# A graph-network kernel of four layers: layer 2's weight product in seven-product form, with the order of its last stage rearranged

## The chip, the cores and the metric

The kernel runs on one core of a Trainium2 chip. The metric is the device time of one execution in microseconds. Before the change three runs took 1876.82, 1876.82 and 1878.27 us.

The engines are named as in the profile: PE is TensorE (matmuls; PEld is its weight loads), DVE is VectorE, ACT is ScalarE, POOL is GpSimd, SP is the engine that issues DMAs. SBUF is the working memory, PSUM the eight banks that TensorE writes its results to.

## The reference

`x` holds 128 graphs of 64 nodes with 256 features, all f32. Four layers follow each other, each with a residual: `x = x + layer(relu(layernorm(x)))`. Layer 0 is two graph convolutions and four LSTM passes, layer 1 two products with batch norms. The change is in the code of layers 2 and 3:

```python
# layer 2: W is (3, 256, 256), adj (64, 64)
adj_0 = jnp.diag(jnp.diagonal(adj)); adj_1 = jnp.triu(adj, k=1); adj_2 = jnp.tril(adj, k=-1)
h = jnp.einsum('bjf,kfo->kbjo', x, W)
out = adj_0 @ h[0] + adj_1 @ h[1] + adj_2 @ h[2] + bias        # per graph
# layer 3: causal attention over the 64 nodes, one head of width 256
q, k, v = jnp.split(x @ Wqkv, 3, axis=-1)
attn = softmax(where(causal, q @ k.T / 16 + adj, -1e30))
out = (attn @ v) @ Wo
```

## The kernel before, in words

The 8192 rows (128 x 64) are cut into 16 supertiles of 512 rows, `s` = 0 to 15; a supertile is four tiles `q` of 128 rows, two graphs in each. The 256 features are two chunks `c` of 128. Layers 0 and 1 run first, up to about 1452 us. Layers 2 and 3 run together in the last stage, supertiles in pairs (an even and an odd one), by the function `rest`.

The order is written out by hand. `rest` calls `at(t, fn, ...)` for every step with a planned time; all steps of all pairs, each pair shifted by `PERIOD`, are sorted by that time and issued in that order. The times only fix the order: each engine runs its own instructions in it, and waits on semaphores for what they need. A step that is issued before another on the same engine therefore holds it up if it has to wait.

For one supertile the steps are:

- `load` (L1196) brings the residual `x1` back from DRAM through SP's queue. `affine` (L1200) finishes layer 1's batch norm on the transposed tiles `y`. `turn` (L1215) transposes them into PSUM, and `turned` adds `x1`: the result is `x2`.
- `norm` (L1226) is layernorm and relu: row statistics on DVE (`stats`), the inverse root on POOL (`root`), the shift on DVE (`shift`), and four relus on ACT, giving `h2`. `biased` (L1260) adds the layer's bias to `x2` on POOL.
- `graphs3` (L1263), four calls, multiplies each graph's 64 rows of `h2` by the three parts of the adjacency, which are packed beside each other (192 columns). Each call has four matmuls on half of the rows of the array and fills two PSUM banks; ACT and DVE copy one each. The result `ag` holds, transposed, three parts `m` of each chunk `c`: `ag[c, m, 512 rows]`.
- `weigh` (L1280) multiplies by the layer's weights: for each tile, six matmuls (two chunks, three parts) with a piece of `ag` as the stationary operand and 256 columns of `wl2[m]` moving. Every f32 matmul appears as two records in the trace. `weighed` adds `x2` and gives `x3`.
- A second `norm` gives `h3`; `h3` and `h3_copy` (L1293, L1301) transpose it. The score product is taken with one combined matrix, in a seven-product form that exists already: `qsum` (L1308) makes sums of the data, `qproduct` (L1319) the seven products with the weight sums `aqk` as the stationary operand, `qcopy` and `qadd` evict them. `hv` (L1344) is the value product.
- `scores` (L1356), `masked`, `largest`, `exps`, `turn_e`, `turned_e` are the softmax; `attend` (L1388) multiplies by the values in two halves of two tiles, and `attended` (L1394) scales the result, adds it into `x3` and, after the second half, issues the output DMA.

The steps of neighbouring supertiles are interleaved so that TensorE has the products of one to do while the other engines work on another. In the steady order of a pair the even and the odd supertile's `graphs3` stand next to each other, then follow the weight products of both, with the odd attention of the pair before, transposes and softmax pieces in between, and then both score products.

PSUM in this stage is one pool, `psum`, of eight banks, in which each new tile takes a bank that earlier steps have been done with, and waits for its last reader. Weights come by DMA in the stage before (`wl2` at L1137, three DMAs of 256 KB). The function `weight_sum` (L307) makes the four sums of a weight matrix that seven-product forms need: `S1 = A21 + A22`, `S2 = S1 - A11`, `S3 = A11 - A21` in A21's place, `S4 = A12 - S2`. It is used for the LSTM, layer 0, layer 1 and `aqk`.

Of the kernel before, what the change touches and what calls it, by code (L numbers as in the profile page):

```python
# [9 lines left out]
F32 = mybir.dt.float32  # L10
AF = mybir.ActivationFunctionType
# [3 lines left out]
P = 128  # L15
# [5 lines left out]
def kernel(ctx: ExitStack, tc: tile.TileContext, a: dict, out: bass.AP):  # L21
# [84 lines left out]
    nc.gpsimd.memset(mhalf, -0.5)  # L106
    eps = const.tile([P, 1], F32, tag="eps", name="eps")
    nc.gpsimd.memset(eps, EPS)
# [770 lines left out]
    def bn_coeffs(name, co, stats, c):  # L879


        prm = con[name]
        mv = lns.tile([P, 2], F32, tag=f"{name}mv{c}", name=f"{name}mv", bufs=1)
        nc.vector.bn_aggr(mv, stats[:, c, :, :].rearrange("p s k -> p (s k)"))
        scale, shift, v = (co[:, k, c : c + 1] for k in range(3))
        nc.gpsimd.tensor_add(v, mv[:, 1:2], eps)
        nc.gpsimd.tensor_tensor(v, v, mhalf[:, :1], ALU.pow)
        nc.gpsimd.tensor_mul(scale, v, prm[:, 1, c : c + 1])
        nc.gpsimd.tensor_mul(shift, mv[:, 0:1], scale)
        nc.gpsimd.tensor_sub(shift, prm[:, 2, c : c + 1], shift)  # L890
# [7 lines left out]
    with tc.tile_pool(name="pz", bufs=1, reuse_waits="tile") as pz:  # L898
# [237 lines left out]
        adj3, smask = adj4[:, 0:3, :], adj4[:, 3, :]  # L1136
        wl2 = [weight(f"wl2_{k}", a["W"][k], late) for k in range(3)]  # L1137
        bl2 = row_bcast("bl2", a["bias"], D, late)
# [4 lines left out]
        wo = weight("wo", a["Wo"], late)  # L1143

        with tc.tile_pool(name="tp", bufs=2, reuse_waits="tile") as tp_:
            tp.append(tp_)
            emit(1e9)
# [30 lines left out]


    PERIOD, HALF = 52.5, SUP // 2  # L1180
    NP = NS // 2
    with tc.tile_pool(name="pc", bufs=2, reuse_waits="tile") as pc, \
            tc.tile_pool(name="pc1", bufs=1, reuse_waits="tile") as pc1:
        events = []

        def rest(s, at, only_pair, t_T, t_n, t_G, t_W, t_h, t_QH, t_S, t_soft, t_E, t_O, end):
            first_, v = s == 0, {}
# [12 lines left out]
            def affine(c):  # L1200
                if s == 1:
                    nc.scalar.activation(y[c], y[c], AF.Identity, bias=co2[:, 1, c : c + 1],
                                         scale=co2[:, 0, c : c + 1])
                    return
                nc.vector.tensor_scalar(y[c], y[c], co2[:, 0, c : c + 1], co2[:, 1, c : c + 1],
                                        op0=ALU.mult, op1=ALU.add)

# [17 lines left out]

            def norm(src, tag, halves, t_rows, t_relu):  # L1226

                def new():
                    v["st"] = pc.tile([P, Q, 6], F32, tag="ln_st", name="ln_st", bufs=4)
                    v["mv"] = pc.tile([P, Q, 2], F32, tag="ln_mv", name="ln_mv", bufs=4)  # L1230
                    v["rn"] = pc.tile([P, 2, Q], F32, tag="ln_rn", name="ln_rn", bufs=4)
                    v[tag] = pc.tile([P, Q, D], F32, tag=tag, name=tag)

                def stats(q):
                    nc.vector.bn_stats(v["st"][:, q, :], v[src][:, q, :])
                    nc.vector.bn_aggr(v["mv"][:, q, :], v["st"][:, q, :])

                def root(qs):
                    rn = v["rn"][:, 0, qs]
                    nc.vector.tensor_scalar_add(rn, v["mv"][:, qs, 1], EPS)  # L1240
                    nc.gpsimd.tensor_tensor(rn, rn, mhalf[:, : qs.stop - qs.start], ALU.pow)  # L1241

                def shift(qs):
                    nc.vector.scalar_tensor_tensor(v["rn"][:, 1, qs], v["mv"][:, qs, 0], -1.0,  # L1244
                                                   v["rn"][:, 0, qs], op0=ALU.mult, op1=ALU.mult)

                def relu(q):
                    nc.scalar.activation(v[tag][:, q, :], v[src][:, q, :], AF.Relu,  # L1248
                                         bias=v["rn"][:, 1, q : q + 1], scale=v["rn"][:, 0, q : q + 1])

                at(t_rows[0] - 0.01, new)
                for q in range(Q):
                    at(t_rows[q // 2] + 0.6 * (q % 2), stats, q)
                for k, qs in enumerate((q2s(0), q2s(1)) if halves else (slice(0, Q),)):
                    at(t_relu[k] - 1.5, root, qs)
                    at(t_relu[k] - 0.1, shift, qs)
                    for q in range(qs.start, qs.stop):
                        at(t_relu[k] + 0.6 * (q - qs.start), relu, q)
# [20 lines left out]

            def weigh(k, q):  # L1280
                if q == 0:
                    v["W"] = two(bank())
                for n in range(3 * KC):
                    c, m = divmod(n, 3)
                    nc.tensor.matmul(v["W"][:, q, :], v["ag"][:, c, m, ts(2 * k + q, P)],  # L1285
                                     wl2[m][:, c, :], start=(n == 0), stop=(n == 3 * KC - 1))

            def weighed(k):
                if k == 0:
                    v["x3"] = pc.tile([P, Q, D], F32, tag="x3", name="x3", bufs=4)  # L1290
                nc.vector.tensor_add(v["x3"][:, q2s(k)], v["x2"][:, q2s(k)], v["W"])

# [15 lines left out]
            def qsum(k):  # L1308
                if k == 1:
                    v["t"] = sums_of.tile([P, 3, 512], F32, tag="th", name="tq").rearrange(  # L1310
                        "p k (n c) -> p (k n) c", c=HALF)
                t = v["t"]
                nc.vector.tensor_sub(t[:, k], *(None, (b_(0, 1), b_(0, 0)), (b_(1, 1), t[:, 1]),
                                                (b_(1, 1), b_(0, 1)), (b_(1, 0), t[:, 2]))[k])
# [4 lines left out]
            def qproduct(name, j):  # L1319
                new = ("q", name) not in v  # L1320
                if new:
                    v["q", name] = bank()[:, :HALF]
                if "qk" not in v:
                    v["qk"] = pc1.tile([P, KC, SUP], F32, tag="qk", name="qk")
                x_ = (b_(0, 0), b_(1, 0), b_(1, 1), *(v["t"][:, k] for k in (4, 1, 2, 3)))[j - 1]
                nc.tensor.matmul(v["q", name], aqk[:, OF[j], :], x_, start=new,  # L1326
                                 stop=(name, j) in (("a", 4), ("b", 3), ("c", 2)), skip_group_check=True)
# [7 lines left out]
            def qdirect(o):  # L1335
                if o == 0:
                    v["qk"] = pc1.tile([P, KC, SUP], F32, tag="qk", name="qk")
                p_ = bank()
# [66 lines left out]
            for c in range(KC):  # L1405
                at(t_T - (2 if first_ else 4.8 if s == 1 else 9) + (0.6 if s != 1 else 0.1) * c, affine, c)
            for k in range(2):
# [5 lines left out]
            if first_:  # L1413
                norm("x2", "h2", True, (t_T + 0.455, t_T + 1.8), (t_T + 3.2, t_T + 4.6))
                for q in range(Q):
                    at(t_T + 7 + 0.7 * q, biased, q)
            else:
                norm("x2", "h2", False, (t_n, t_n + 1.2), (t_n + (11.9 if s % 2 and s > 1 else 4.1),))
                for q in range(Q):
                    at(t_n + (18 if s % 2 else 10.5) + 0.7 * q, biased, q)  # L1420
            for k in range(4):
                at(t_G + 0.8 * k, graphs3, *((k % 2, k // 2) if first_ else (k // 2, k % 2)))
            for k in range(2):
                for q in range(2):
                    at(t_W[k] + 2.6 * q, weigh, k, q)
                at(t_W[k] + 5.3, weighed, k)
            norm("x3", "h3", False, (t_W[0] + 5.8, t_W[1] + 5.8), (t_W[1] + 8.8,))
            for c in range(KC):
# [35 lines left out]
            for k in range(2):  # L1464
                at(t_O + 0.86 * k, attend, k)
                at(t_O + 0.86 * k + 0.9, attended, k)

        for i in range(NP):
            t0, first_, end = PERIOD * i, i == 0, i == NP - 1

            def at(t, fn, *args, t0=t0):
                events.append((t0 + t, len(events), fn, args))

            rest(2 * i, at, i, -8.6 if first_ else -40.2, -38.3, 0, (7.0, 12.6), 29.0, 32.6, 40.0, 42.7,
                 46.3 if end else 48.46, 50.4 if end else 50.85, False)
            if first_:
                at(-7.6, weight_product, 2, wo, wvo)
                for k in range(8):
                    at(3.0 + 0.5 * k, qk_weights, k)
            rest(2 * i + 1, at, i, -3.0 if first_ else -27.6, 1.5 if first_ else -25.4, 12.3 if first_ else 3.5, (17.8, 26.5), 39.1,  # L1480
                 (42.0, 45.4, 48.7, 49.6, 52.1) if end else 42.0, 46.7 if end else 48.9,
                 49.5 if end else 59.5, 53.0 if end else 64.7, 53.8 if end else 75.6, end)
        for _, _, fn, args in sorted(events, key=lambda e: e[:2]):
# [40 lines left out]
```

## Time and profile before

| | us |
|---|---|
| median of three runs | 1876.82 |
| the profiled execution, its own time | 1876.78 |
| its span, first to last instruction | 1875.1 |
| last stage, from the first `graphs3` to the end | 413.6 (1461.46 to 1875.1) |
| of this: first pair, to the next pair's `graphs3` | 51.33 |
| six pairs, 1512.79 to 1818.09 | 305.30 |
| last pair and tail | 57.01 |
| PE busy in these six pairs | 305.30 of 305.30 |

The last four rows come from the trace's view by windows. A line of the profile that names a group gives the source line, the engine, the operation, `out<-in` with the names of the tiles, the sizes (partitions x elements), the count, and then the busy time, the mean length of one in ns, and the idle time ahead of it with what ended most of it. A line of the trace in order of time begins with start and length in us; a bracket at its end is the idle time ahead of it and who ended it. [...] the distance from start to start is its price in a stream.

### The profile page before, as it was taken

The page shows a single profiled execution, that of the slowest core. Times are in us where ns is not written, and L with a number is a line of the kernel's source. Part 1 is how long each engine was busy: PE and PEld are TensorE (multiplying, and loading weights), DVE is VectorE, ACT ScalarE, POOL GpSimd, SP SyncE. Part 2 cuts the span into 40 slices and gives each one's busy share as a digit, 9 for nine tenths or more (in the row PEclk, how much of TensorE's full clock was granted, in tenths as well). Part 3 has the DMA queues.
Part 4 walks back from the last instruction along what each step waited for, and adds up shares of the span by engine and source line. Part 5 has one row for each costly group of instructions (what it writes and reads, how often), then busy time and mean ns, then how long its engine had stood idle before and what let it go on. Part 6 is the DMA issues. An engine that isn't in the chain of part 4 may idle for free.

```text
span 1875.1 us, 19841 instructions
## 1 busy us (share of the span) xinstructions
PE 1853.9 (99%) x7080; PEld 1168.8 (62%) x7080; DVE 1129.4 (60%) x2254; ACT 925.7 (49%) x1594; POOL 645.4 (34%) x553
## 2 busy tenths in 40 slices
PE   8999999999999999999999999999999999999999
PEld 7997444444445666666444444566444788888887
DVE  6775777634546435445633333588876776667674
ACT  6776666534435334433533333378685434433442
POOL 4451422443424433422442222267353412211220
PEclk9999999999999999999999999999999999999999
DMA  4110001000001000000000000243200111111101
GB/s 146 57 57 1 1 1 29 16 1 0 1 0 45 1 0 1 1 1 1 23 0 0 1 0 0 102 132 116 71 1 2 44 46 46 35 46 46 46 23 34
DMA packets 50642, 54.86 MB, mean 29 GB/s; under 512 B 3184, under 2 KB 45936, under 8 KB 50544
## 3 DMA queue, kind: packets, MB, share of 16 engines
q1 hardware_dynamic: 50096, 53.30, 8.9%
q8 instruction: 56, 0.92, 0.2%
q14 instruction: 42, 0.34, 0.1%
q10 hardware_dynamic: 448, 0.30, 0.0%
HBM read 36.55 MB, written 17.04 MB: 29 GB/s over the span
## 4 chain that ended last, share of the span: by engine, by line
PE 93%; DVE 3%; POOL 1%; ACT 1%; DMA 1%; issue 1%; SPq 0%; ACTq 0%; DVEq 0%; POOLq 0%
PE ps L686 34%; PE ps L692 19%; PE ps L1285 8%; PE ps L930 5%; PE ps L1047 4%; PE ps L1350 3%; PE ps L392 3%; PE ps L402 3%; PE ps L1326 2%; PE ps L431 2%; PE ps L1273 2%; PE ps L1360 2%; PE ps L1391 1%; PE ps L623 1%; PE ps L1298 1%; PE ps L579 1%
## 5 line engine op out<-in xcount | busy, mean ns | idle before, releaser
L708 DVE TENSOR_TENSOR gate<-gate,ps 128x512 f32<-128x512 f32 (+2 forms) x378 | 223.9, 620 | 449.0 <-PE ps L692 367.7
L686 PE MATMUL ps<-tx,wih 128*128 128x512 f32 (+2 forms) x996 | 441.2, 541 | 1.9 <-ACT gate L711 1.0
L686 PE MATMUL ps<-hT,wih 128*128 128x512 f32 (+2 forms) x756 | 338.5, 541 | 0.0
L711 ACT COPY gate<-ps 128x512 f32<-128x512 f32 (+2 forms) x252 | 134.5, 534 | 378.4 <-PE ps L692 325.4
L686 PEld LDWEIGHTS ps<-tx,wih 128*128 128x128 f32 x996 | 188.4, 190 | 188.2 <-issue 128.2
L704 ACT ACTIVATE gate<-gate,lbias 128x512 f32<-128x512 f32 (+2 forms) x252 | 216.7, 860 | 160.0 <-DVE gate L708 160.0
L692 PE MATMUL ps<-h,whh 128*128 128x512 f32 (+2 forms) x576 | 256.6, 527 | 0.0
L686 PEld LDWEIGHTS ps<-hT,wih 128*128 128x128 f32 x756 | 143.6, 190 | 141.6 <-issue 79.4
L692 PE MATMUL ps<-th,whh 128*128 128x512 f32 (+2 forms) x432 | 192.5, 527 | 0.0
L731 POOL TENSOR_TENSOR gate<-gate 128x1024 f32<-128x1024 f32 (+2 forms) x36 | 71.9, 2019 | 297.5 <-ACT gate L704 297.5
L1285 PE MATMUL ps<-wl,ag 128*128 128x256 f32 x768 | 172.1, 380 | 0.0
L692 PEld LDWEIGHTS ps<-h,whh 128*128 128x128 f32 x576 | 109.4, 190 | 100.2 <-issue 76.5
L1285 PEld LDWEIGHTS ps<-wl,ag 128*128 128x128 f32 x768 | 143.4, 190 | 20.2 <-ACT ag L1278 1.8
L731 POOL TENSOR_TENSOR cell<-gate 128x1024 f32<-128x1024 f32 (+2 forms) x36 | 79.4, 2225 | 174.8 <-ACT gate L704 174.8
L1241 POOL TENSOR_TENSOR ln_rn<-ln_rn,mhalf 128x4 f32<-128x4 f32 (+1 forms) x33 | 32.8, 995 | 300.8 <-DVE ln_rn L1240 300.3
L692 PEld LDWEIGHTS ps<-th,whh 128*128 128x128 f32 x432 | 82.1, 190 | 75.2 <-issue 57.4
L1248 ACT ACTIVATE h<-x,ln_rn 128x256 f32<-128x256 f32 x128 | 68.2, 593 | 103.3 <-DVE ln_rn L1244 103.3
L731 POOL TENSOR_TENSOR cell<-gate,cell 128x1024 f32<-128x1024 f32 (+2 forms) x31 | 62.8, 2044 | 110.2 <-ACT gate L704 110.2
L711 DVE COPY gate<-ps 128x512 f32<-128x512 f32 (+2 forms) x126 | 78.6, 624 | 20.8 <-PE ps L692 20.8
L704 ACT ACTIVATE gate<-ps,lbias 128x512 f32<-128x512 f32 (+2 forms) x126 | 79.6, 631 | 3.8 <-PE ps L692 1.0
L736 ACT ACTIVATE gate<-cell 128x1024 f32<-128x1024 f32 (+2 forms) x72 | 68.0, 951 | 26.1 <-POOL cell L731 26.1
L648 DVE TENSOR_TENSOR tx<-hT,tx 128x512 f32<-128x512 f32 (+2 forms) x70 | 57.7, 825 | 13.8 <-PE ps L686 10.2
(236 smaller groups left out, 2933.8 us busy)
## 6 DMA issues: line engine op xcount, KB each, us to landing
xt<-in_x_dram SPq DMA_DIRECT2D x30, 512.0 KB, 4.2
x1d<-xt SPq DMA_DIRECT2D x16, 512.0 KB, 3.0
x<-x1d SPq DMA_DIRECT2D x16, 512.0 KB, 4.9
out_dram<-x SPq DMA_DIRECT2D x15, 512.0 KB, 3.0
wih<-in_WihT_dram SPq DMA_DIRECT2D x16, 256.0 KB, 4.8
whh<-in_WhhT_dram SPq DMA_DIRECT2D x12, 256.0 KB, 4.8
xt<-in_x_dram SPq DMA_DIRECT2D x6, 128.0 KB, 3.2
wl<-in_W_dram SPq DMA_DIRECT2D x3, 256.0 KB, 3.6
```

What stands on the lines that cost most here:

```text
L648: yield nc.vector.tensor_sub(t[k], *((b[1][0], b[0][0]), (b[1][1], t[0]), (b[1][1], b[1][0]), (b[0][1], t[1 % len(t)]))[k])
L686: nc.tensor.matmul(wide(p_[:, :N]), wih[0][:, OF[k], gi, :], x_, start=first_, stop=(j == 0), skip_group_check=True)
L692: nc.tensor.matmul(p_[:, :N], whh[0][:, OF[k], gi, :], h_, start=False, stop=True, skip_group_check=True)
L704: nc.scalar.activation(to, r[bank_][:, :N] if bank_ else to, fn, bias=lbias[:, l, m : m + 1])
L708: nc.vector.tensor_add(slot(n, hc), slot(n, hc), r[bank_][:, :N])
L711: op(slot(n, hc), r[bank_][:, :N])
L731: fn(*((t["G"] if isinstance(t, dict) and "G" in t else st["c"])[:, n, :, : st["N"]] for t in tiles))
L736: nc.scalar.activation(o_, c, AF.Tanh)
L930: nc.tensor.matmul(r[name], con["w1"][:, OF[j], g, :], x_, start=new, stop=(name, j) in (("a", 4), ("b", 3), ("c", 2)), skip_group_check=True)
L1047: nc.tensor.matmul(banks[name], w2[:, OF[j], k, :], x_, start=(new and k == 0), stop=(k == 1), skip_group_check=True)
L1248: nc.scalar.activation(v[tag][:, q, :], v[src][:, q, :], AF.Relu, bias=v["rn"][:, 1, q : q + 1], scale=v["rn"][:, 0, q : q + 1])
L1285: nc.tensor.matmul(v["W"][:, q, :], v["ag"][:, c, m, ts(2 * k + q, P)], wl2[m][:, c, :], start=(n == 0), stop=(n == 3 * KC - 1))
```

## The change

Layer 2's weight product of supertiles 1 to 15 takes a seven-product form. The two halves `n` of a supertile's rows and the two input chunks `c` are the blocks of the data, the two input and two output halves of 128 the blocks of the weights; each block holds the three adjacency parts, and a product sums over them. The four data sums (`gsum`, 128 x 768 each) are made on POOL, two of them in place. They are the stationary operand, 128 columns of weights (or weight sums) the moving one. A product `gproduct` is six matmuls (two tiles, three parts). Products 1, 6, 7 and 4 accumulate one after the other into one bank `a`, which is read after each of them; `b` and `c` hold the others. `gevict` and `gadd` put the quarters of `x3` together on DVE. Supertile 0 takes the old sums, in matmuls of 128 columns (`gdirect`).

With it:

- `wl2` becomes one tile of seven blocks, loaded by four DMAs; three of its weight sums are made on POOL during layer 1's second product, the last one after supertile 0 has read what it overwrites.
- PSUM is split in this stage: one bank for `a`, two for `b` and `c`, five for the rest. The score product uses the same `a` and `bc` banks.
- The even and the odd `graphs3` are two groups now: the even one, then two even weight products, then the odd one.
- The second half of the odd attention moves behind the fourth weight product of the odd supertile, the first half ahead of the even one's. The even attention's second eviction moves behind the `graphs3` evictions.
- In `norm`, adding epsilon and the shift move from DVE to POOL. `qsum` moves from DVE to POOL. `affine` moves from DVE to ACT and is planned earlier, except for supertile 0. The transposes of the next pair move to later places: among the score products.
- `qk` takes the place of `wqkv`, the data sums that of `wT`, both read for the last time before.

```diff
-        wl2 = [weight(f"wl2_{k}", a["W"][k], late) for k in range(3)]
+        wl2 = late.tile([P, 7, 3, P], F32, tag="wl2", name="wl2")
+        for o in range(2):
+            for c in range(2):
+                nc.sync.dma_start(wl2[:, 2 * o + c], a["W"].rearrange(
+                    "m (c p) (o n) -> o c p m n", c=2, o=2)[o, c])
...
+        for k in range(4):
+            if k != 2:
+                at(B + 60 + 5.16 * k, weight_sum, wl2, k)
...
+    new_banks(a=1, bc=2, psum=5)
...
                 def root(qs):
-                    rn = v["rn"][:, 0, qs]
-                    nc.vector.tensor_scalar_add(rn, v["mv"][:, qs, 1], EPS)
-                    nc.gpsimd.tensor_tensor(rn, rn, mhalf[:, : qs.stop - qs.start], ALU.pow)
+                    rn, nm = v["rn"][:, 0, qs], v["rn"][:, 1, qs]
+                    n = qs.stop - qs.start
+                    nc.gpsimd.tensor_add(rn, v["mv"][:, qs, 1], eps[:, :n])
+                    nc.gpsimd.tensor_tensor(rn, rn, mhalf[:, :n], ALU.pow)
+                    nc.gpsimd.tensor_mul(nm, v["mv"][:, qs, 0], rn)
+                    nc.gpsimd.tensor_mul(nm, nm, mone[:, :n])
...
-            def weigh(k, q):
-                if q == 0:
-                    v["W"] = two(bank())
-                for n in range(3 * KC):
-                    c, m = divmod(n, 3)
-                    nc.tensor.matmul(v["W"][:, q, :], v["ag"][:, c, m, ts(2 * k + q, P)],
-                                     wl2[m][:, c, :], start=(n == 0), stop=(n == 3 * KC - 1))
+            def g_(c, n):
+                return v["ag"][:, c, :, ts(n, HALF)]
+
+            def gsum(k):
+                if k == 0:
+                    v["t2"] = late.tile([P, 3 * KC, D], F32, tag="wT", name="tg")
+                t1, t2 = v["t2"][:, 0:3], v["t2"][:, 3:6]
+                if k == 0:
+                    nc.gpsimd.tensor_sub(t1, g_(0, 1), g_(0, 0))
+                elif k == 1:
+                    nc.gpsimd.tensor_sub(g_(0, 1), g_(1, 1), g_(0, 1))
+                elif k == 2:
+                    nc.gpsimd.tensor_add(t2, g_(0, 1), g_(0, 0))
+                else:
+                    nc.gpsimd.tensor_sub(g_(1, 0), g_(1, 0), t2)
+
+            def gproduct(name, j):
...
+                for p_ in range(2):
+                    for m in range(3):
+                        nc.tensor.matmul(v["g", name][:, p_, :], x_[:, m, ts(p_, P)], wl2[:, OF[j], m, :],
...
-                nc.vector.tensor_sub(t[:, k], *(None, (b_(0, 1), b_(0, 0)), (b_(1, 1), t[:, 1]),
+                nc.gpsimd.tensor_sub(t[:, k], *(None, (b_(0, 1), b_(0, 0)), (b_(1, 1), t[:, 1]),
...
             for k in range(2):
-                at(t_O + 0.86 * k, attend, k)
-                at(t_O + 0.86 * k + 0.9, attended, k)
+                at(t_O[k], attend, k)
+                at(t_O[2 + k], attended, k)
...
-            rest(2 * i, at, i, -8.6 if first_ else -40.2, -38.3, 0, (7.0, 12.6), 29.0, 32.6, 40.0, 42.7,
-                 46.3 if end else 48.46, 50.4 if end else 50.85, False)
+            rest(2 * i, at, i, -8.6 if first_ else -14.5, -12.5, 0,
+                 (7.0, 9.6, 12.2, 14.8) if first_ else (7.0, 8.3, 9.6, 10.9, 12.2, 13.5, 15.8),
+                 (3.3, 5.2, 7.1, 9.0), (12.5, 17.5) if first_ else (17.4, 15.3), 20.5, 25.75, 31.4, 40.0, 42.7,
+                 46.3 if end else 48.46, (50.4, 51.26, 51.3, 52.16) if end else (50.85, 51.71, 51.75, 55.4), False)
...
-            rest(2 * i + 1, at, i, -3.0 if first_ else -27.6, 1.5 if first_ else -25.4, 12.3 if first_ else 3.5, (17.8, 26.5), 39.1,
+            rest(2 * i + 1, at, i, -3.0 if first_ else -6.05, 1.5 if first_ else -5.2,
+                 12.25 if first_ else 9.0, (17.85, 19.6, 20.9, 22.2, 23.5, 24.8, 26.9),
+                 (16.0, 17.0, 18.0, 22.0) if first_ else (12.3, 14.2, 16.1, 22.0), (31.4, 30.6), 35.3, 39.1,
```

## The prediction

> **What bounds the kernel now.** I read the page first: busy time, then the chain that ended last, then TensorE in order of time over one period of the last stage, the only stage that the change rearranges.
>
> ```profile
> PE 1853.9 (99%) x7080; PEld 1168.8 (62%) x7080; DVE 1129.4 (60%) x2254; ACT 925.7 (49%) x1594; POOL 645.4 (34%) x553
> PEclk9999999999999999999999999999999999999999
> PE 93%; DVE 3%; POOL 1%; ACT 1%; DMA 1%; issue 1%; SPq 0%; ACTq 0%; DVEq 0%; POOLq 0%
> ```
>
> TensorE is busy 99% of the span at the full granted clock and holds 93% of the chain. In this kernel a microsecond is gained only by fewer TensorE microseconds, and lost by any wait of TensorE. The period of one pair of supertiles:
>
> ```profile
> 1614.55 5.47 PE L1273 MATMUL ps<-adj,h 64*128 64x192 f32 x64
> 1619.95 5.45 PE L1285 MATMUL ps<-wl,ag 128*128 128x256 f32 x24
> ...
> 1626.55 10.53 PE L1285 MATMUL ps<-wl,ag 128*128 128x256 f32 x48
> 1636.91 1.89 PE L1391 MATMUL ps<-hw,eT 128*128 128x256 f32 x8
> ...
> 1652.05 1.25 PE L1298 MATMUL ps<-ident,h 128*128 128x128 f32 x8
> 1653.13 1.95 PE L1360 MATMUL ps<-h3T,qk 128*128 128x128 f32 x16
> 1654.91 1.03 PE L1326 MATMUL ps<-h3T,aqk 128*128 128x256 f32 x4
> ...
> 1665.44 5.47 PE L1273 MATMUL ps<-adj,h 64*128 64x192 f32 x64
> ```
>
> Columns: start, length, engine, line, operation, operands, count of records. [...] Each f32 matmul is two records. The period is 1665.44 - 1614.55 = 50.89 us, with no marked idle. A 256-column record costs (1636.91 - 1626.55) / 48 = 0.216 us; a 128-column record with a new stationary tile each time (the scores) costs (1654.91 - 1653.13) / 16 = 0.1115, 1.79 / 16 = 0.112 in other periods. I take 0.1117.
>
> **Matmuls removed and added.** Before, a supertile's weight product has 24 matmuls, 48 records: 48 x 0.216 = 10.36 us. After, supertiles 1 to 15 have 7 products x 2 token tiles x 3 parts = 42 matmuls of 128 columns, 84 records: 84 x 0.1117 = 9.38 us, 0.98 less. Supertile 0 does the old sums in 48 matmuls of 128 columns: 96 x 0.1117 = 10.72, 0.36 more. Together 15 x -0.98 + 0.36 = **-14.3 us**. One eighth fewer columns would be 19.4 us; a quarter of it is eaten because two 128-column records cost 0.223 against 0.216.
>
> [...] The scores row is this very stream, in f32, and shows 0.112. I take the row.
>
> **Waits that the change adds on TensorE, per pair.** PSUM is split into one bank for the running accumulation, two for the others, and five for all else. During the even supertile's adjacency products one of the five is held by the second attention half, whose eviction now stands on VectorE behind four copies, so these products rotate in four banks.
>
> ```profile
> 1615.51 0.48 ACT L1278 COPY ag<-ps 128x384 f32<-128x384 f32 x1 [4.21 <-PE ps L1273]
> 1615.55 0.56 DVE L1278 COPY ag<-ps 128x384 f32<-128x384 f32 x1 [0.87 <-PE ps L1273]
> ```
>
> Against the first call's start (1614.55) the ACT copy ends at 1.44, the VectorE copy at 1.56. A call takes 5.40 / 8 = 0.675. The third call is ready at 1.35 and starts at about 1.51 (a released TensorE started 0.05 to 0.1 late): 0.16 lost. The first product reads what the third call made; its copies now end at about 3.07, TensorE is ready at 2.87: 0.27 lost. Before, the other supertile's adjacency products covered this. The odd group waits about 0.11 for an ACT copy, since four relus (2.07) and three exps (0.39 each) are queued ahead of it. Sum 0.54 per pair. Bounds: 0 if the copies land first; 1.5 if each odd copy is late by a whole exp.
>
> What goes with the old order: 0.1 before the first weight records (5.28 for 24 against 5.18) and 0.2 in the L1298 group (1.08 against 0.87), which now has transposes ahead of it: -0.3.
>
> **GpSimd's queue.** It takes over four data sums per supertile (128x768), the four sums of the attention product, and the norm's root and shift.
>
> ```profile
> L591 POOL TENSOR_TENSOR xt<-xt,h 128x512 f32<-128x512 f32 x24 | 30.1, 1276 | 0.0
> L1261 POOL TENSOR_TENSOR x<-x,bl 128x256 f32<-128x256 f32 x64 | 48.1, 777 | 10.7 <-ACT h L1248 10.7
> L1241 POOL TENSOR_TENSOR ln_rn<-ln_rn,mhalf 128x4 f32<-128x4 f32 x31 | 31.4, 1014 | 296.5 <-DVE ln_rn L1240 296.5
> L610 POOL TENSOR_TENSOR ln_rn<-ln_rn 128x4 f32<-128x4 f32 x16 | 3.2, 201 | 1.3
> ```
>
> From 256 (0.70 to 0.78) and 512 (1.28) columns a 768-column sum is about 1.83. Walking the queue from the even adjacency start: four even sums 2.3 to 9.6, four bias adds (0.73) to 12.5, three odd sums to 17.9. The odd sixth product needs the third at 20.6: 2.7 us spare. The root is now 0.2 + 1.01 + 0.2 + 0.2 with gaps, 1.85 against about 1.45; its relus end near 23.1, their transposes start at 24.7. Of the fourth sums the odd one is done at 22.9, needed at 25.5. All covered, and the price beyond the cover is the excess, once per pair.
>
> Contention is the unknown. This case shows it on VectorE:
>
> ```profile
> 1645.42 0.42 DVE L1313 TENSOR_TENSOR tq<-h3T,tq 128x256 f32<-128x256 f32 x1
> ...
> 1655.30 0.94 DVE L1313 TENSOR_TENSOR tq<-h3T 128x256 f32<-128x256 f32 x1
> ```
>
> The second ran beside GpSimd's bias adds. [...] By the worst such row (1.60 for 512 columns beside VectorE sums) a 768 sum would be 2.3, and the spare 2.7 would be overdrawn by 0.6. [...] I take 1.83.
>
> **Moves at nothing.** VectorE loses four sums (0.42 to 0.94) and two affines (0.53) a supertile and gains seven evictions (about 0.4) for two of 0.68; each eviction of the single accumulation bank must end within one product (1.34) and its queue leaves 0.1 to 0.7. ACT gains the affines (0.76) in stretches where it idles. The closest meeting: the copy of the transposed exponentials waits behind three row statistics and ends as attention is ready; 0.1 per pair is set down. The weight load is four DMAs instead of three, long landed; three weight sums of about 1 us fall in GpSimd's idle (27.0 us over seven pairs) during the second product.
>
> **SP's queue.** The second half of the odd attention moves from 1636.9 (22.4 us into the period) to about 27 us. Its output store now stands on SP ahead of the next pair's two loads, which came at 4 and 17 us of a period before and are needed from 34.9. Released at 28.8, a load lands 4.9 later by its row, at 33.7: 1.2 spare. [...] if a whole store (3.0) comes first, it lands at 36.7, 1.8 late, of which TensorE sees 1.4, since the copies of h3T queue behind it on VectorE with 0.4 spare. Nearest is the lone-load row; I set down 0.1 and keep 0 and 1.4.
>
> **The sum against the profiled execution** (1876.78; span 1875.1; the median of the runs, 1876.82, is the same). Six middle pairs: -1.96 + 0.54 + 0.1 (eT) + 0.1 (load) - 0.3 = -1.52, so -9.1. First pair: -0.62; +0.3 root; +0.3 adjacency; the sixth product waits on GpSimd, where one more weight sum stands ahead of two data sums, +0.87; the 0.79 wait for h3T goes: +0.1. Last pair: -1.96 + 0.54 - 0.1, and +0.4 because no transposes cover the slower root there: -1.1. In all -10.1: **1866.7 us**.
>
> **Rivals.** (1) *No new wait*, 0.14: copies land before TensorE needs their banks: -14.3 - 7 x 0.3 + 0.4 = -16.0, 1860.8. For: no wait in the present trace is over 0.3 us in the middle pairs; against: 1.44 after 1.35. (2) *Evictions pace TensorE*, 0.20: or the late load does: each of eight adjacency calls waits 0.15 and one product 0.2, or the load's 1.4 is seen, in seven pairs: 1866.7 + 9.8 = 1876.5. For: four banks for eight copies, three 512 KB transfers at once; against: VectorE's copies repeat every 0.49. (3) *GpSimd ends on the other side*, 0.09: with sums of g us the odd third sum ends at 5.2 + 7g. The 1.52 gain is gone when that passes 20.6 by 1.52, at g = 2.42; at 2.6 it passes by 2.8, a loss of 1.3 per pair: 1876.8 + 7 x 1.3 - 1 = 1885. For: the 1.60 row; [...] The built program does hold 630 + 48 matmuls, so doing nothing is no case.
>
> **Numbers.** Forecast's own case, 0.55: 1863 to 1871. Cases (1) and most of (2) belong in the range: 1860 to 1876. A change is told from none beyond 0.2%, 3.8 us: faster below 1873.1. Case (2) is split 0.09 faster, 0.10 same, 0.01 slower, case (3) 0.02 same, 0.07 slower: faster 0.78, same 0.12, slower 0.10.
>
> **What would show it.** Right: the period at 49.2 to 49.5; product records at 0.112; TensorE idle with releaser L1286's copies, about 0.5 per pair, in the third call and the first product. Wrong: product records over 0.12; idle released by GpSimd's data sums, which would then be over 2.2 us each; or accumulating products waiting for their evictions.

## The result and the profile after

The changed kernel takes **1868.99 us** (median of five runs, 1868.89 to 1869.76), the kernel before beside it 1877.69 (1876.82 to 1878.27): ratio 0.9955, 95% interval 0.9941 to 0.9970. It is faster by 0.45%; the forecast was 1866.7, in a range from 1860 to 1876.

The profiled execution took 1868.99, its span is 1867.2, against 1876.78 and 1875.1 before.

| | before | after | forecast change | change |
|---|---|---|---|---|
| up to the last stage | 1461.46 | 1460.82 | 0 | -0.64 |
| first pair | 51.33 | 51.57 | +0.1 | +0.24 |
| six pairs | 305.30 | 298.28 | -9.1 | -7.02 |
| last pair and tail | 57.01 | 56.53 | -1.1 | -0.48 |
| span | 1875.1 | 1867.2 | -10.1 | -7.9 |

The first pair needs a caution. The view by windows, the first pair before, then the first pair and the six middle pairs of the changed kernel, whose window ends 0.02 early (length, then busy time of PE, PEld, DVE, ACT and POOL, the granted clock of TensorE, and DMA):

```profile
1461.46:1512.79 51.33, 50.37 (x297) 43.22 (x297) 37.70 (x98) 22.86 (x52) 19.42 (x30) 1.00 0.04 11
```

```profile
1460.82:1512.39 51.57, 51.39 (x380) 47.47 (x380) 28.97 (x78) 24.07 (x52) 32.98 (x54) 0.97 0.04 11
1512.39:1810.65 298.26, 297.71 (x2281) 277.78 (x2280) 194.79 (x505) 136.37 (x336) 192.51 (x241) 1.00 0.13 43
```

The granted clock of 0.97 comes from a stretch of 3.4 us at 0.50, which the profiled execution of the kernel before did not have. The middle pairs ran at 1.00 in both, so the versions are compared by their periods below.

The page of the changed kernel, busy time and the new group of product records:

```profile
PE 1846.8 (99%) x7668; PEld 1179.0 (63%) x7668; DVE 1097.1 (59%) x2175; ACT 943.4 (51%) x1622; POOL 817.2 (44%) x777
...
L1314 PE MATMUL ps<-wl,ag 128*128 128x128 f32 x900 | 108.3, 276 | 0.6
```

TensorE still fills the span; GpSimd has taken over 172 us of work and VectorE has lost 32. TensorE in order of time, from the first adjacency call of a period:

```profile
1562.11 3.17 PE L1281 MATMUL ps<-adj,h 64*128 64x192 f32 x32
1565.37 2.92 PE L1314 MATMUL ps<-wl,ag 128*128 128x128 f32 x24
1568.22 3.05 PE L1281 MATMUL ps<-adj,h 64*128 64x192 f32 x32
1571.19 2.94 PE L1314 MATMUL ps<-wl,tg 128*128 128x128 f32 x24
...
1611.82 1.41 PE L1281 MATMUL ps<-adj,h 64*128 64x192 f32 x14
```

Read from start to start, since a length runs past the next start (1565.37 + 2.92 = 1568.29, and the next group starts at 1568.22), the period is 1611.82 - 1562.11 = 49.71, 1.18 less, where 1.52 was forecast. The 64 adjacency records of a pair took 1619.95 - 1614.55 = 5.40 in one group before. Now the even 32 take 3.26 and the odd 32 take 2.97, 6.23 together. The product records have the price that was taken. Later in the period 36 of them take 1581.97 - 1577.96 = 4.01, 0.1114 each:

```profile
1577.96 4.18 PE L1314 MATMUL ps<-wl,ag 128*128 128x128 f32 x36
1581.97 2.84 PE L1314 MATMUL ps<-wl,tg 128*128 128x128 f32 x24
```

So the loss sits in and around the adjacency groups, and no line there carries a bracket. It shows in another view, the waits of the weight loads (PEld), here for the six middle pairs of the changed kernel: engine, line, who it waited for, us in all, times, longest.

```profile
PEld ps L1314 <- ACT ag L1286: 2.1, 6, 0.4
PEld ps L1281 <- issue: 2.0, 6, 0.3
PEld ps L1314 <- issue: 1.3, 6, 0.2
PEld ps L1281 <- ACT ag L1286: 1.2, 6, 0.2
```

Two of the four rows say "issue": TensorE stood and waited for nothing that the profile shows. One is the step into the even adjacency group, one the step out of the odd group into products. The other two are the even third call (0.2) and the first product behind the even group (0.4). The same view of the kernel before, over its six middle pairs, had been there to be read:

```profile
PEld ps L1273 <- issue: 2.3, 7, 0.3
PEld ps L1298 <- ACT h L1248: 1.4, 6, 0.2
PEld ps L1285 <- ACT ag L1278: 1.3, 6, 0.2
```

The step into a group is there (0.3), and the step out, with the copies named as releaser; the middle row is the old wait of the L1298 transposes.

**A ledger of one period.** Each run of equal records is set against its count times the undisturbed price (0.1117 at 128 columns, 0.216 at 256, 0.0813 for an adjacency record, since two run side by side, 0.007 apart, and a pair of them comes every 0.163). What is over, in us:

| | before | after |
|---|---|---|
| steps into and out of the (even) group | 0.39 | 0.39 |
| even group: third call waits for banks | 0 | 0.31 |
| first product waits for the third call's copies | 0 | 0.13 |
| steps into and out of the odd group | no such group | 0.39 |
| odd group: third call waits for a bank | 0 | 0.18 |
| transposes of h3 (L1298) | 0.21 | 0 |
| sum | 0.60 | 1.40 |

A group that nothing holds up still costs 0.39: the last 256-column record ahead of it is followed after 0.309 instead of 0.216 (0.09), the group itself takes 0.20 over its records, and the first product record behind it takes 0.10 more. Products: 2 x (9.38 - 10.37) = -1.97. With +0.80 that is -1.17, the measured change.

### The profile page after: what moved, and what is told of

It reads as the page before. It is cut to its first block, busy times and chain, and to the rows that moved or that the text cites. A ratio compares the mean times of both kernels' runs of the same rounds, so it can differ in the third digit from the quotient of the medians.

```text
span 1867.2 us, 21317 instructions
## 1 busy us (share of the span) xinstructions
PE 1846.8 (99%) x7668; PEld 1179.0 (63%) x7668; DVE 1097.1 (59%) x2175; ACT 943.4 (51%) x1622; POOL 817.2 (44%) x777
## 4 chain that ended last, share of the span: by engine, by line
PE 94%; DVE 2%; POOL 1%; ACT 1%; issue 1%; DMA 0%; SPq 0%; DVEq 0%; POOLq 0%; ACTq 0%
PE ps L688 34%; PE ps L694 19%; PE ps L1314 7%; PE ps L932 5%; PE ps L1049 4%; PE ps L394 3%; PE ps L404 3%; PE ps L1401 3%; PE ps L1281 3%; PE ps L433 2%; PE ps L1377 2%; PE ps L1411 2%; PE ps L1442 1%; PE ps L625 1%; PE ps L1349 1%; PE ps L581 1%
## 5 line engine op out<-in xcount | busy, mean ns | idle before, releaser
L1314 PE MATMUL ps<-wl,ag 128*128 128x128 f32 x900 | 108.3, 276 | 0.6
L1314 PEld LDWEIGHTS ps<-wl,ag 128*128 128x128 f32 x900 | 104.2, 192 | 3.3 <-ACT ag L1286 2.5
L733 POOL TENSOR_TENSOR cell<-cell,gate 128x1024 f32<-128x1024 f32 (+2 forms) x31 | 65.5, 2135 | 0.4
```

Source lines behind the costliest of these rows:

```text
L733: fn(*((t["G"] if isinstance(t, dict) and "G" in t else st["c"])[:, n, :, : st["N"]] for t in tiles))
L1314: nc.tensor.matmul(v["g", name][:, p_, :], x_[:, m, ts(p_, P)], wl2[:, OF[j], m, :], start=new and p_ == m == 0, stop=m == 2 and (name, j) ...
```

## The experiments

Theory A: TensorE pays about 0.39 us for each group of 64-row adjacency matmuls among its 128-row ones, in and out, whoever waits. Theory B, the rival: all of the loss is waiting for PSUM banks and their evictions, and goes with them. The medians, the period in the profiled execution, and the ratio to the kernel before:

| | median us | period us | ratio, 95% interval |
|---|---|---|---|
| before, measured beside each | 1876.63 to 1877.69 | 50.89 | |
| changed | 1868.99 | 49.71 | 0.9955 (0.9941 to 0.9970) |
| two_groups_before | 1881.84 | 51.63 | 1.0025 (1.0015 to 1.0035) |
| three_groups | 1870.35 | 49.93 | 0.9964 (0.9952 to 0.9977) |
| full_rows | 1884.15 | 51.70 | 1.0035 (1.0021 to 1.0049) |
| six_banks | 1868.85 | 49.79 | 0.9956 (0.9944 to 0.9969) |
| a1_first | 1873.34 | 50.36 | 0.9979 (0.9973 to 0.9986) |
| no_waits | 1872.20 | 50.25 | 0.9972 (0.9961 to 0.9982) |
| no_waits2 | 1862.93 | 49.10 | 0.9926 (0.9914 to 0.9939) |
| one_group | 1867.16 | 49.55 | 0.9944 (0.9931 to 0.9956) |
| one_group2 | 1860.53 | 48.71 | 0.9915 (0.9901 to 0.9928) |
| order_only | 1885.92 | 52.13 | 1.0046 (1.0033 to 1.0059) |
| double_sum | 1875.64 | 50.59 | 0.9993 (0.9985 to 1.0001) |

**Two groups in the kernel before.** One planned time is moved:

```diff
-            rest(2 * i + 1, at, i, -3.0 if first_ else -27.6, 1.5 if first_ else -25.4, 12.3 if first_ else 3.5, (17.8, 26.5), 39.1,
+            rest(2 * i + 1, at, i, -3.0 if first_ else -27.6, 1.5 if first_ else -25.4, 12.3 if first_ else 9.5, (17.8, 26.5), 39.1,
```

> The kernel before with one edit: in pairs 1 to 7 the second supertile's four adjacency calls run behind the first quarter of the first supertile's weight product instead of directly behind the first supertile's calls. Same instructions, eight PSUM banks, no seven-product form. Theory A (a change of TensorE between 128-row and 64-row matmuls costs about 0.2 us each way, whatever waits there are): the period grows by 0.39 from 50.89 to about 51.28, and the kernel by 7 x 0.39 = 2.7, to about 1880.4. Theory B (the loss in the changed kernel's second group is a wait for PSUM banks and their evictions): with eight banks nothing waits, the period stays at 50.9 and the time within 0.5 us of 1877.7.

The four odd calls are planned 0.8 apart, so the next quarter of the product, planned at 9.6, fell between the first and the second: three groups, not two. TensorE of that kernel:

```profile
1615.42 2.87 PE L1273 MATMUL ps<-adj,h 64*128 64x192 f32 x32
1618.22 2.86 PE L1285 MATMUL ps<-wl,ag 128*128 128x256 f32 x12
1621.01 0.92 PE L1273 MATMUL ps<-adj,h 64*128 64x192 f32 x8
1621.86 2.86 PE L1285 MATMUL ps<-wl,ag 128*128 128x256 f32 x12
1624.64 2.22 PE L1273 MATMUL ps<-adj,h 64*128 64x192 f32 x24
1626.80 0.44 PE L1381 MATMUL ps<-ident,sc 128*128 128x128 f32 x2
```

Eight records take 0.85 where 0.65 is their price, 24 take 2.16 where 1.95 is, 32 take 2.80 where 2.60 is, and 12 product records between two groups 2.79 where 12 x 0.216 = 2.59. The overhead is the same for 8, 24 and 32 records (and for 64 before), with eight banks and nothing to wait for: a price per group. Two groups more at 0.39 are 0.78; the last one steps out into transposes, where the second record is 0.05 less late than among products; the period is 0.74 longer. Theory B had said 0.

**Three groups in the changed kernel.** The fifth product goes between the second and the third odd call:

```diff
-at(t_G + (... else 0.05 if s % 2 else 0.8) * k, graphs3, ...)
+at(t_G + (... else (0.05 * k + 1.7 * (k // 2)) / max(k, 1) if s % 2 else 0.8) * k, graphs3, ...)
```

> The changed kernel with the odd supertile's four adjacency calls split in two and two: the fifth product (b5) stands between them. One more group per pair. Theory A (each group costs 0.39 us for the change of matmul rows and back): +0.39, less the 0.17 that the third odd call now waits for its bank, +0.22 per pair in pairs 1 to 7, the period 49.93 instead of 49.71, 1870.5. Theory B (the second group loses time to evictions): the split gives the evictions 1.3 us more, so 0.17 to 0.5 per pair is gained, the period 49.2 to 49.5, 1865.5 to 1867.8.

The period is 49.93, as theory A said, and the time 1870.35. The 0.18 of waiting went, and the third group's 0.39 outweighed it: 0.22 more in all.

**Full rows.** The odd groups are multiplied as 128-row matmuls, both blocks at once:

```diff
+                if s % 2:
+                    full = [bank()[:, : 3 * P].rearrange("p (k n) -> p k n", k=3) for _ in range(2)]
+                    for q in range(2):
+                        nc.tensor.matmul(full[q], v["h2"][:, 2 * k + q, ts(c, P)], adj3, start=True, stop=True)
...
+                    return
```

> The changed kernel with the odd supertiles' adjacency products as 128-row matmuls: each takes both 64-row blocks at once against the block-diagonal matrix, 384 columns, so the two halves no longer run side by side. 16 records of about 0.324 us instead of 32 that take 2.60 together: +2.58. Theory A (the loss is the change of matmul rows): the odd group's steps in and out, 0.39 together, vanish, as does its bank wait of 0.17: +2.0 per pair, period 51.7. Theory B (any group of matmuls whose results others evict pays on entry and exit): the steps stay, +2.4, period 52.1.

```profile
1616.96 3.17 PE L1289 MATMUL ps<-adj,h 64*128 64x192 f32 x32
1620.22 2.92 PE L1322 MATMUL ps<-wl,ag 128*128 128x128 f32 x24
1622.97 5.33 PE L1279 MATMUL ps<-adj,h 128*128 128x384 f32 x16
1628.13 2.84 PE L1322 MATMUL ps<-wl,tg 128*128 128x128 f32 x24
```

16 records of 384 columns take 1628.13 - 1622.97 = 5.16, 0.3226 each where 0.324 was expected, so nothing on top; the products behind take 2.68 for 24, their bare price. The 64-row group in the same kernel, at 1616.96, keeps its steps. The same copies and the same evictions follow both kinds of group, so the copies aren't what costs the 0.39: it comes with the 64-row matmuls. Whether the change of rows or the running of two row tiles side by side is charged, no run here separates. The period, 51.70, is theory A's.

**Six banks, and the products exchanged.** Two edits aimed at the waits:

```diff
-    new_banks(a=1, bc=2, psum=5)
+    new_banks(a=1, bc=1, psum=6)
-                    v["q", name] = bank("a" if name == "a" else "bc")[:, :HALF]
+                    v["q", name] = bank({"a": "a", "b": "bc", "c": "psum"}[name])[:, :HALF]
```

> The changed kernel with six general PSUM banks instead of five: the non-accumulating products of the weight stage share one bank, and in the attention product the short-lived one takes a general bank. Theory A: only the waits inside the groups go, up to 0.30 in the even group (one of the six is still held by the second attention half) and 0.17 in the odd one; the steps into and out of each group stay at about 0.2 each. Period 49.25 to 49.5, time 1865.7 to 1867.6. Theory B (banks are the whole loss): the 0.39 of the second group goes as well, period 48.9 or less, 1863.

```diff
-zip(t_W, (("c", 2), ("a", 1), ("b", 5), ...
+zip(t_W, (("a", 1), ("c", 2), ("b", 5), ...
-(0, gevict, 0, 0, "c"), (1, gadd, 0, 0, "a")
+(0, gevict, 0, 0, "a"), (1, gadd, 0, 0, "c")
```

> The changed kernel with the first two products exchanged: the one that reads the first adjacency call's sums runs ahead of the one that reads the third call's. If the step from the even group to its first product holds 0.16 us of waiting for the third call's two copies on top of the change of matmul rows, as the records read (0.415 here against 0.252 behind the odd group), the step falls to 0.25 and the period by 0.16 to about 49.55: 7 x 0.16 = 1.1, 1867.9. If the whole step is a wait for copies, it falls to 0.11 and the period to 49.4. If it is all the change of rows, nothing moves.

Both expectations of the time failed, though the waits that were aimed at went. With six banks the odd group has 0.20 over its records instead of 0.38, and the even one 0.54 instead of 0.66; but the odd fifth product now waits 0.37 for the second product's eviction, since both use the one bank left. With the products exchanged the step behind the even group falls from 0.415 to 0.253, and the odd first product now waits where nothing waited: 0.78 are lost there. TensorE and then VectorE of that kernel:

```profile
1630.10 2.16 PE L1314 MATMUL ps<-wl,ag 128*128 128x128 f32 x17 [0.51 <-DVE x L1339]
```

```profile
1629.62 0.42 DVE L1339 TENSOR_TENSOR x<-x,ps 128x256 f32<-128x256 f32 x1 [0.57 <-PE ps L1314]
```

The fourth even product and the first odd product use the single accumulation bank one after the other. In the changed kernel the second odd product stands between them and covers the eviction. In both kernels a product that had no wait of its own had been the cover of another's.

**No waits, two groups.** Six banks, a general bank for the odd second product, the exchange for even supertiles only, and the second attention half evicted ahead of the adjacency copies (its planned time 55.4 becomes 52.49):

> The changed kernel with three edits against its waits: six general PSUM banks (the odd supertile's short-lived product takes a general bank, so the accumulating one is free), the even supertile's first two products exchanged, and the second attention half evicted ahead of the adjacency copies instead of behind them. The 0.31 in the even group, the 0.13 at its first product and the 0.17 in the odd group should go, and the two groups keep 0.39 each (theory A): period 49.10, 7 x 0.61 = 4.3 less, the first pair up to 1.5 less; 1863 to 1865. Theory B (no fixed cost of a group): period 48.7 or less, below 1861.

The period was 50.25, a miss on the slow side. The even group is free of waits (2.80), but the even fifth product waits 1.17. VectorE of that kernel:

```profile
1617.68 2.51 DVE L1286 COPY ag<-ps 128x384 f32<-128x384 f32 x4 [1.75 <-PE ps L1281]
1620.10 0.41 DVE L1342 TENSOR_TENSOR x<-x,ps 128x256 f32<-128x256 f32 x1
```

The second product was ready before 1617; the eviction that frees its bank stands behind the four odd copies. The next version plans that `gadd` 0.73 earlier, ahead of the odd calls:

```diff
-                    at(t_W[t] + 1.35, fn, *args)
+                    at(t_W[t] + (0.62 if t == 1 and not s % 2 else 1.35), fn, *args)
```

> The version with two groups, six banks and exchanged products once more, with one addition of the first attention-free kind: the eviction of the even supertile's second product stands on VectorE ahead of the odd adjacency copies instead of behind them, since the third product needs its bank. That wait was 1.17 us per pair. Theory A: with it gone only the two groups' 0.39 each remain, period 50.25 - 1.15 = 49.10; 7 x 0.6 under the changed kernel, 1863 to 1865. If a period below 48.8 comes out, the groups have no fixed cost and theory A falls.

```profile
1610.08 2.87 PE L1281 MATMUL ps<-adj,h 64*128 64x192 f32 x32
1612.88 2.94 PE L1314 MATMUL ps<-wl,ag 128*128 128x128 f32 x24
1615.75 2.87 PE L1281 MATMUL ps<-adj,h 64*128 64x192 f32 x32
1618.55 2.94 PE L1314 MATMUL ps<-wl,tg 128*128 128x128 f32 x24
```

49.10 as theory A said. Both groups take 2.80, 0.20 over 2.60, with every wait gone.

**One group.** The same with the odd calls directly behind the even ones. The odd turn runs 2.05 earlier in plan, its relus ahead of the copies, and its load, affine and bias adds are moved to fit:

```diff
-            rest(2 * i + 1, at, i, -3.0 if first_ else -6.05, 1.5 if first_ else -5.2,
-                 12.25 if first_ else 9.0, ...
+            rest(2 * i + 1, at, i, -3.0 if first_ else -8.1, 1.5 if first_ else -6.1,
+                 12.25 if first_ else 3.2, ...
```

> The version before this (six banks, no waits) with the odd supertile's adjacency calls directly behind the even one's, as in the kernel before the change: its turn, statistics, root and relus run earlier for it. Theory A: one group less per pair, -0.39, period 48.7, 7 x 0.39 = 2.7 less than the version with two groups: 1860.5 to 1862. Against it: eight copies in a row on ScalarE and VectorE, and the odd relus end 0.1 us ahead of the first copy by the timeline; if they are late the gain is lost and the period stays at 49.1 or above.

The first try had a period of 49.55: with the even products exchanged the fifth stands next to the second and waits 0.84 for its bank. The second try leaves the products in the changed kernel's order:

> The version with one group and six banks once more, with the even supertile's products in the order of the changed kernel (second, first, fifth), so that the first product covers the eviction of the second; the wait of 0.84 before the fifth product goes. Theory A: one group's 0.39 is all that is left, period 49.55 - 0.84 = 48.71, 7 x 1.0 under the changed kernel, 1861 to 1863, and 0.39 per pair under the version with two groups. If GpSimd's sums, which now start 1 us later than the adjacency products end early, hold the sixth product, the period stays above 49.

```profile
1607.82 5.47 PE L1281 MATMUL ps<-adj,h 64*128 64x192 f32 x64
1613.22 2.94 PE L1314 MATMUL ps<-wl,ag 128*128 128x128 f32 x24
1616.00 2.84 PE L1314 MATMUL ps<-wl,tg 128*128 128x128 f32 x24
```

48.71, and **1860.53 us**, the fastest version here. 64 records take 5.40, 0.20 over 5.20, as 32 did: one group is paid once. Against the kernel before the period is 2.17 less: 1.97 from the arithmetic and 0.21 from the wait at the transposes.

**Order only.** All supertiles with 24 matmuls of 256 columns in the changed order, without data sums. (The third weight sum is left in place and overwrites A21 after supertile 0, so the later supertiles multiply by another block; the amount of work is the same.)

> The changed kernel with every supertile's weight product in 24 matmuls of 256 columns, as before the change, in the changed order; no seven-product form, no data sums, one eviction per half. The price of the arithmetic alone: 15 x 0.98 - 0.36 = 14.3 us more on TensorE than the changed kernel, 1883.3, if the seven-product form (its data sums on GpSimd, its seven evictions) adds no wait of its own; the order alone would then cost 6 us against the kernel before. If the form brings waits that this version is spared (0.2 per pair or more), 1882 or less.

1885.92, 2.6 above the expected time. The period is 2.42 over the changed kernel's: 1.97 for the records, less 0.13 at the first product, whose wait went, and 0.58 for a wait that this version adds itself: its last eviction stands on VectorE ahead of the copies of h3T. Neither expectation had a wait on this side. By the ledger, the arithmetic is worth 1.97 per pair, and the rearranged order costs 0.80 of it; without its own wait this version would be 52.13 - 0.58 - 50.89 = 0.66 over the kernel before, which is the 0.80 less the 0.13.

**GpSimd's cover.** The first data sum of each supertile is computed twice:

> The changed kernel with the first data sum of every supertile computed twice (1.82 us more for GpSimd per supertile, 3.6 to 3.8 by the odd supertile's third sum). By the timeline of the changed kernel that third sum ends at 1580.2 and its product starts at 1583.3: a cover of 3.07. If the sums bound nothing until the cover is used up, TensorE waits 0.7 to 0.9 per pair: period 50.4 to 50.6, first pair 2 to 4 longer, 1876 to 1879. If GpSimd already sets the pace, the whole 3.7 per pair shows: period 53.4, above 1895. If the cover is larger than it looks, 1870.

Period 50.59, 0.88 more; 1875.64, just under the expected span of times. The odd third sum ends 3.80 us later in the period. A cover of 3.07, as the timeline of the changed kernel showed, leaves 0.73 of that, and 0.88 is seen; with a late record behind the wait, 0.10 at the sixth product in the first pair of the changed kernel, it would be 0.83, an estimate. Rival (3) would have needed sums slow enough to use up that cover.

## Why the prediction was right or wrong

**Class and size.** Faster, and inside the range, but 2.3 us short of the point forecast. The period that was named as a sign of being right, 49.2 to 49.5, did not appear: it is 49.71.

**Matmuls removed and added: right.** The record price was 0.1114 to 0.1117 for the products, so two 128-column records against one of 256 behave as the scores row showed (0.112).

**Waits that the change adds: right in sum, half wrong in the causes.** 0.54 was forecast and 0.61 measured (0.31 + 0.13 + 0.18, each rounded). The even group lost 0.31 at its third call where 0.16 was set down, and 0.13 behind it instead of 0.27. The odd wait, 0.18 against 0.11, has another cause than the one given. That the three came so near in sum is in part luck. ScalarE in the changed kernel:

```profile
1569.17 0.48 ACT L1286 COPY ag<-ps 128x384 f32<-128x384 f32 x1 [0.37 <-PE ps L1281]
1569.82 0.48 ACT L1286 COPY ag<-ps 128x384 f32<-128x384 f32 x1 [0.17 <-PE ps L1281]
```

The four relus and three exps were done 0.37 before the first copy could start. The third call needs a bank that this copy leaves at 1569.65, and TensorE is there at 1569.62. With six banks and the same queue on ScalarE the wait was gone.

**What goes with the old order: here the prediction failed.** It counted -0.3, of which 0.1 "before the first weight records" (5.28 for 24 against 5.18). That 0.1 was the tail of the step out of a 64-row group. It belongs to the group, stayed, and came a second time with the second group. So -0.3 should have been -0.21 + 0.39 = +0.18. The prediction had the step in front of it: a group of 64 records took 5.40, and 0.675 per call was read off that as if it were all price. The runs put these steps at 0.39 us in and out. In seven pairs this term was wrong by 7 x 0.48 = 3.4 us, more than the 2.3 that are missing; other errors, below, made up for the rest.

**Two small charges that were not seen.** The copy of the transposed exponentials (0.1) and the load (0.1) cost nothing: TensorE shows no excess at the attention, at the turns or at h3T in a middle pair. With these the per-pair sum closes: -1.52 + 0.48 (steps) + 0.07 (waits) - 0.2 = -1.17.

**First and last pair.** The last pair lost 0.55 at the transposes of h3 for the slower root, where 0.4 was forecast, and missed its -1.1 mainly by the same steps. In the first pair the sixth product waited 0.26 instead of 0.87, and 0.35 of the wait for h3T stayed. Against that, supertile 0's adjacency group took 4.74 where 3.12 was measured before and 0.3 of loss forecast. Two things add up in this. With six banks (six_banks, no_waits, one_group2) the group took 3.18, with five and the full clock (a1_first, full_rows, order_only, double_sum) 3.82 to 3.83: the five banks cost 0.70. The rest, 0.92, goes with the granted clock, which was 0.50 from 1461.6 to 1465.0, inside this group: a pair of adjacency records came every 0.320 us there instead of 0.163. The executions of three_groups, no_waits2 and one_group have the same 3.4 us, and there the group took 4.24 to 4.83. What lowered the clock is not shown. At the full clock the first pair would by this be near 50.65 (a1_first, at the full clock, has 50.67), 0.7 shorter than before, where +0.1 was forecast: that the table has +0.24 is luck, and the profiled execution would fall short of the forecast by 1.3 instead of 2.2. The 0.64 ahead of the last stage was not forecast either; over all versions that stage begins between 1460.8 and 1461.6.

**GpSimd: right.** The 768-column sum took 1.81 to 1.82 us (1.83 was set down, the author's estimate), in a stage where VectorE ran beside it, so the contention of rival (3) did not come. In layer 1 of the kernel before, GpSimd's 512-column sum (L1035) took 1.60 beside a VectorE sum that took 1.57 instead of 0.69; what separates the two cases is not shown. The odd third sum ended at 1580.24, and its product, the second twelve of the 24 records at 1581.97, started at 1583.31: 3.07 spare, 2.7 forecast.

```profile
1578.43 1.81 POOL L1302 TENSOR_TENSOR tg<-ag 128x768 f32<-128x768 f32 x1
```

**Rival (2)** had TensorE paced by evictions in all eight calls; two calls of eight waited. **Rival (1)**, no wait, is what no_waits2 built, and even then the steps remained: 1862.93 where the rival had 1860.8.

## What to carry to other kernels

When a reordering splits a group of row-tiled matmuls, count its steps in and out as work: read them off as what a group takes over its records' price, for two group sizes (here 0.20 over it for 8 records and for 64, 0.39 with the steps outside). Before an edit takes a wait away, ask which wait the present order covers: three versions here removed the wait they aimed at and made one at the next user of the same bank. A stalled TensorE may carry no bracket in order of time (none at L1281 in the changed kernel's middle pairs, where the weight loads show 0.33); look at the waits of the weight loads too.

## What the runs showed of the hardware

- 64-row groups among 128-row matmuls cost 0.39 us, 0.20 of it over the group's own records: 0.85 where 0.65 is the price of 8 (two_groups_before), 5.40 where 5.20 is the price of 64 (kernel before). Each way it is about 0.09 of standing and then one record that comes 0.10 late: 0.309 instead of 0.216 into the group and 0.267 instead of 0.163 behind its first pair; 0.253 instead of 0.156 out of it and 0.320 instead of 0.216 behind the first product record (kernel before).
- A wait of TensorE cost more than its length. In the changed kernel the sixth product of the first pair (1484.30) starts 0.371 after the record ahead of it instead of 0.112, and the next record follows after 0.213: another 0.10. Behind a wait at the transposes of h3 (kernel before, 1499.88) it was 0.06: 0.165 instead of 0.109. The 0.10 in the group steps is of the first size.
- Behind the third calls, which wait for banks in the changed kernel, the two 64-row halves run on staggered: 0.124 apart in the even group and 0.019 in the odd one, instead of 0.007. Each half still gives a record every 0.163.
